# Half products of keys and values moved between the turns of an autocorrelation, and three reorderings, in a two-layer Flamingo block

## The chip, the cores and the metric

The kernel runs on one core of a Trainium2 chip. The metric is the device time of one execution in microseconds (us); the kernel before takes 3443.58 us, the median of three runs (3438.86 to 3445.33).

The engines are named as in the profile: PE is TensorE's matmul, PEld its weight load, DVE is VectorE, ACT is ScalarE, POOL is GpSimd, SP is SyncE. Everything is computed in float32.

## The reference, cut to what matters

The input `x` is 8 batches of 256 rows of 1024, the context `ctx` likewise. Four residual steps follow one another, each on the layer norm of the current `x` and each weighted by the tanh of a gate:

```python
x = x + tanh(g_xattn[0]) * autocorrelation(layernorm(x), ctx, ctx)
x = x + tanh(g_ffn[0])   * lora_ffn(layernorm(x), ...)
x = x + tanh(g_xattn[1]) * attention(layernorm(x), ctx, ctx, mask, wq, wk, wv, wo)
x = x + tanh(g_ffn[1])   * fourier_ffn(layernorm(x), ...)
```

The first is the one that the change is mostly about. For each column it correlates queries and keys over the 256 positions with a Fourier transform, takes the eleven largest lags, weighs them with a softmax, and sums the values shifted by these lags. The second is a dense layer with a low-rank part whose rank is picked for each row by a small gate. The third is attention with 32 query heads on 8 key heads; its keys and values are `ctx @ wk` and `ctx @ wv`, which depend on nothing computed before. The fourth is a dense layer whose weights are folded with a Fourier part.

## The kernel before, in words

The batches are done in two passes of four. In each pass the four steps follow one another on the same eight tiles `xt` of 128 rows, which stay on the chip.

**Products by sevens.** The large matrix products are done by a scheme of seven products in the place of eight (`left_operands` and `right_operands` make sums of quarters; `combine` and `add_product` put the results together). The order of the seven is `SEVEN = (1, 2, 6, 7, 4, 5, 3)`. Products 6, 5, 3 and 7 need sums of weights; in the first pass these are made on the chip (DVE for keys, POOL for values) and stored, and in the later ones they are loaded.

**Keys and values beside the autocorrelation.** `keys_values` computes the keys and values of the third step ahead of time. It is a generator: each of its steps is one half product, eight PE instructions of 128x256. A block of 512 rows has four units (two of keys, two of values) of 14 half products, and a pass has two blocks: 112 half products. In the first pass `fold_last_layer`, which folds the weights of the fourth step, comes behind them with 17 further steps. `autocorrelation` takes steps from this stock with `fill(n)`; what is left when it ends is run without anything beside it. PE has work to do in a fill whatever the autocorrelation waits for. The sums of a product's halves for a key end in a rotary embedding (`rope`, three DVE operations and one on POOL).

**Turns.** The autocorrelation runs over eight half batches (a batch, and 512 of its 1024 columns), one in each call of `turn`, and a ninth call finishes the last. A turn holds two things that belong to different half batches. For its own half batch it does the discrete Fourier transforms of keys and queries (`dft`, L412), their products (`products`, DVE L428 to L431 and POOL L432 to L436, which gives `re` and `im`), the correlation back (`correlation`, L561 and L562, in two parts of two column groups each), and the lags and weights of each of four column groups (`lags`), which end in a tile `both` (POOL L552 and L553). For the half batch before, it transposes `both` (L515), transforms it, multiplies it with the transforms of the values, and goes back to positions: this is `back(l)`, whose two calls each do two matmuls of `inv2` (L531) on the tiles `er`, `ei`, `odr` and `odi`, and add the result to two tiles of `x` (DVE L371). In the order that the products leave POOL these four are `er`, `ei`, `odr`, `odi` (the page names the first two `re` and `im`).

**Order.** Each engine goes through its instructions in the order in which the built program has them. That order follows the source, but a scheduler of the framework moves instructions of one engine past others where it expects a wait, so a step that the source has later isn't always later on its engine. DMAs are nearly all issued from SP's queue[...]. PSUM has two buffers for the products of keys and values, four for `dft`, one for correlations, one for `po` and `pt`.

**Names of the steps.** Ahead of the first turn a pass does `late()`, which loads tiles 2 to 7 of `x` (six DMAs of 512 KB); `normalize(0, 1)`, the statistics of batch 0; and `sums`, which makes the normalized columns and the sums and differences that the transforms start from. After the first turn come the statistics of the other batches, `normalize(1, BP)`.

**The gate of the second step.** `lora_ffn` takes two tiles of rows at a time. `prepare` normalizes and transposes a tile, multiplies it by the low-rank matrix and the gate (`pa`, L623), and masks the result (`xa`, DVE L630 to L642); `turned` transposes `xa` on PE (`px`, L647) and copies it to `xaT`; `left` makes the sums of the tile pair; `project` is the seven products (L670) of the pair before.

Of the kernel before, what the change touches and what calls it, by code (L numbers as in the profile page):

```python
# [11 lines left out]
F32 = mybir.dt.float32  # L12
# [3 lines left out]
ALU = mybir.AluOpType  # L16
# [3 lines left out]
P = 128  # L20
# [9 lines left out]
R0 = 64  # L30
# [9 lines left out]
KH = KC // 2  # L40
# [6 lines left out]
def flamingo_kernel(ctx: ExitStack, tc: tile.TileContext, a: dict, out: bass.AP):  # L47
    nc = tc.nc
# [21 lines left out]
    tg_x, ntg_x = ([t[:, i, 0:1] for i in range(2)] for t in (tg, ntg))  # L70
# [37 lines left out]
    def big_tile(group, shape, name):  # L108
        return big.tile([P, *shape], F32, tag=group, name=name)
# [93 lines left out]
    def left_operands(eng, q, s1, s2, s4):  # L203


        eng.tensor_add(s1, q[1][0], q[1][1])
        eng.tensor_sub(q[1][0], q[0][0], q[1][0])
        eng.tensor_sub(s2, s1, q[0][0])
        eng.tensor_sub(s4, q[0][1], s2)
        return {1: q[0][0], 2: q[0][1], 3: s4, 4: q[1][1], 5: s1, 6: s2, 7: q[1][0]}  # L210
# [158 lines left out]
    def residual(xs, ps, g):  # L369

        nc.vector.scalar_tensor_tensor(xs, ps, g, xs, ALU.mult, ALU.add)  # L371
# [12 lines left out]
    def autocorrelation(p, xt, pools, beside, late):  # L384
        c1, w1, w2, ps_dft, ps_cor, ps_out = pools

        def fill(n):
            for _ in range(n):
                next(beside, None)
# [83 lines left out]
        def turn(this, before, coming):  # L473


            after = None
            if this:
                b, cols, end, qe, qo, ke, ko = this
                if coming:
                    coming = loads(coming)  # L480
                kr_ps, ki_ps = dft((KCE, ke)), dft((KSE, ko), (NYQ, ke))


                kr, ki, kn = sb("kr"), sb("ki"), sb("kn")
                nc.scalar.copy(kr, kr_ps)
                nc.scalar.copy(kn, kr_ps)
                nc.scalar.activation(ki, ki_ps, AF.Copy, scale=pair)
                nc.scalar.copy(kn[0:1, :], ki_ps[0:1, :])
                re, im = sb("re"), sb("im")
                products(spectrum((CE, SE), (qe, qo)), kr, ki, kn, re, im, False)  # L490
                fill(2)

            if this:
                vr_ps, vi_ps = dft((KCO, ko)), dft((KSO, ke))
                vr, vi = sb("vr"), sb("vi")
                nc.scalar.copy(vr, vr_ps)
                nc.scalar.copy(vi, vi_ps)

                nc.vector.scalar_tensor_tensor(
                    kr[0:1, :], end[0:1, :], 2.0 * S, kr[0:1, :], ALU.mult, ALU.add  # L500
                )
                if coming:
                    after = sums(*coming)
                fill(2)
            last = not this
            if before:
                if last:
                    fill(3)
                b_cols, b_tiles, (bkr, bki, bkn, bvr, bvi, both) = before

                wt = []
                for t in range(2):
                    pt = ps_out.tile([P, HALF], F32, tag="out", name="pt")
                    for c in range(4):
                        nc.tensor.transpose(pt[:, c * P : (c + 1) * P], both[:, t, c, :], ident)  # L515
                    wt.append(one(f"wt{t}"))
                    nc.scalar.copy(wt[t], pt)
                    fill(2 if last else 1)
                er, ei = sb("re"), sb("im")
                products(spectrum((CE, SE), wt), bkr, bki, bkn, er, ei, True)  # L520
                fill(2 if last else 1)
                odr, odi = one("odr"), one("odi")
                products(spectrum((CO, SO), wt[::-1]), bvr, bvi, bvr, odr, odi, True)
                fill(3 if last else 1)

            def back(l):

                if before:
                    po = ps_out.tile([P, HALF], F32, tag="out", name="po")
                    for i, (k, sp) in enumerate(((0, er), (3, odi)) if l == 0 else ((1, ei), (2, odr))):  # L530
                        nc.tensor.matmul(po, inv2[:, k, :], sp, start=(i == 0), stop=(i == 1))  # L531
                    residual(b_tiles[0][:, b_cols], po, tg_x[0])
                    residual(b_tiles[1][:, b_cols], po, ntg_x[0] if l else tg_x[0])
                    fill(1)

            if last:
                back(0)
                back(1)
                return None, None
            w = big_tile("xn", [4, S], "w")  # L540
            cor = correlation(re, im, 0)
            fill(1)
            back(0)
            cor += correlation(re, im, 2)
            for c in range(2):
                lags(w[:, c, :], cor[c])
            fill(1)
            back(1)
            for c in range(2, 4):
                lags(w[:, c, :], cor[c])  # L550
            both = big_tile("xn", [2, 4, P], "both")
            nc.gpsimd.tensor_add(both[:, 0], w[:, :, 0:P], w[:, :, P:S])  # L552
            nc.gpsimd.tensor_sub(both[:, 1], w[:, :, 0:P], w[:, :, P:S])  # L553
            return after, (cols, xt[b * 2 : b * 2 + 2], (kr, ki, kn, vr, vi, both))
# [12 lines left out]
        def lags(w, cor):  # L567


            top = w2.tile([P, 16], F32, tag="top", name="top", bufs=4)  # L570
            left = w2.tile([P, S], F32, tag="left", name="left", bufs=1)
            took = w2.tile([P, S], F32, tag="took", name="took", bufs=1)
            nc.vector.max(top[:, 0:8], cor)
            neg = w2.tile([P, 1], F32, tag="neg", name="neg", bufs=4)
            nc.vector.tensor_scalar(neg, top[:, 0:1], -1.0, None, ALU.mult)
            ex = w2.tile([P, S], F32, tag="ex", name="ex")
            nc.scalar.activation(ex, cor, AF.Exp, bias=neg)
            nc.vector.match_replace(left, top[:, 0:8], cor, NEG)
            nc.vector.max(top[:, 8:16], left)
            nc.vector.memset(top[:, 11:16], NEG)  # L580
            nc.vector.match_replace(took, top[:, 8:16], left, NEG)
            tot = w2.tile([P, 1], F32, tag="tot", name="tot", bufs=4)
            nc.vector.scalar_tensor_tensor(
                w, took, NEG, ex, ALU.is_equal, ALU.mult, accum_out=tot
            )
            nc.vector.reciprocal(tot, tot)
            nc.scalar.activation(w, w, AF.Copy, scale=tot)

        order = [(b, h) for b in range(BP) for h in range(2)]
        first = loads(order[0])  # L590
        inv = c1.tile([P, 2, S], F32, name="inv")
        nc.sync.dma_start(inv, a["dft_inv"])
        inv2 = c1.tile([P, 4, P], F32, name="inv2")
        nc.sync.dma_start(inv2, a["lag_inv"])
        late()
        fill(6 if p == 0 else 4)
        normalize(0, 1)
        this, before = sums(*first), None
        fill(7 if p == 0 else 3)
        for i in range(len(order)):  # L600
            this, before = turn(this, before, order[i + 1] if i + 1 < len(order) else None)
            if i == 0:
# [4 lines left out]
    def lora_ffn(xt, w0, make_w0, ag, bl, beside):  # L607

        with (
# [32 lines left out]
                    nc.vector.tensor_scalar(xa[:, r], pa[:, r], past[:, i : i + 1], None, ALU.mult)  # L642
                return xnT, xa

            def turned(xnT, xa):
                px = ps_s.tile([R0 + 1, P], F32, tag="s", name="px")
                nc.tensor.transpose(px, xa, ident)  # L647
                xaT = w2.tile([R0 + 1, P], F32, tag="xaT", name="xaT", bufs=4)
                nc.scalar.copy(xaT, px)
                return xnT, xaT  # L650

            def left(m, first, second):
                q = [[s[0][:, k * KH : (k + 1) * KH, :] for k in range(2)] for s in (first, second)]
                s = [w2.tile([P, KH, P], F32, tag=f"s{i}", name=f"s{i}") for i in (1, 2, 4)]
                ops = left_operands(nc.gpsimd if m else nc.vector, q, *s)
                neg = w2.tile([R0 + 1, P], F32, tag="neg", name="neg")
                nc.vector.tensor_scalar(neg, second[1], -1.0, None, ALU.mult)
                return ops, first[1], second[1], neg

            def project(m, ops, up, low, neg):  # L660
                x = [
# [26 lines left out]
            pending = None  # L688
            for m in range(TT // 2):
                norm = norm_stats(xt[m * 2 : m * 2 + 2])  # L690
                got = [prepare(m * 2 + i, norm) for i in range(2)]
                steps = project(*pending) if pending else iter(())
                for _ in range(2):
                    next(steps, None)
                got = left(m, *(turned(*x) for x in got))
                if pending is None and make_w0:
                    w0.update(make_w0())
                for _ in steps:
                    pass
                pending = (m, *got)  # L700
            beside(w2, ps_t, "t")
            for _ in project(*pending):
                pass
# [444 lines left out]
    for p in range(NPASS):  # L1148
        ga, gb = ("a", "b") if p % 2 == 0 else ("b", "a")
        xt = [xpool.tile([P, D], F32, tag="x", name="x") for t in range(TT)]  # L1150
        with (
# [22 lines left out]
            steps = beside()  # L1174
# [178 lines left out]
```

## Time and profile before

| | before |
|---|---|
| median of three runs | 3443.58 us |
| the profiled execution | 3440.27 us |
| its span in the profile | 3438.5 us |
| mean granted clock of TensorE | 0.984 |
| PE busy | 3335.6 us (97%) |
| DVE, POOL, ACT busy | 2227.5, 1413.8, 860.5 us |
| autocorrelation of the first pass, first transform to last `po` | 36.95 to 396.5 us |
| of the second pass | 1771.37 to 2112.6 us |

A line of the list of waits has the engine and line that waited, what ended the wait, the sum in us, how often, and the longest. A line of the timeline has its start, its duration (of all its instructions together), the engine, line and operation, the tiles and how many; in brackets stands the idle time before it and what ended that. A line of the table of stretches has, for each engine, the busy time and the number of instructions, then the clock granted to TensorE (1.00 is full), the share of DMA and GB/s.

### The profile page before, as it was taken

The page shows a single profiled execution, that of the slowest core. Times are in us where ns is not written, and L with a number is a line of the kernel's source. Part 1 is how long each engine was busy: PE and PEld are TensorE (multiplying, and loading weights), DVE is VectorE, ACT ScalarE, POOL GpSimd, SP SyncE. Part 2 cuts the span into 40 slices and gives each one's busy share as a digit, 9 for nine tenths or more (in the row PEclk, how much of TensorE's full clock was granted, in tenths as well). Part 3 has the DMA queues.
Part 4 walks back from the last instruction along what each step waited for, and adds up shares of the span by engine and source line. Part 5 has one row for each costly group of instructions (what it writes and reads, how often), then busy time and mean ns, then how long its engine had stood idle before and what let it go on. Part 6 is the DMA issues. An engine that isn't in the chain of part 4 may idle for free. (4 is left out here: it accounts for less than half of the span.)

```text
span 3438.5 us, 36954 instructions
## 1 busy us (share of the span) xinstructions
PE 3335.6 (97%) x12784; PEld 2287.7 (67%) x12784; DVE 2227.5 (65%) x4181; ACT 860.5 (25%) x2061; POOL 1413.8 (41%) x1259
## 2 busy tenths in 40 slices
PE   7899989999999999999999999999999999999998
PEld 6576545877766776776466666477777776776754
DVE  7677555877777666666557675456666666666562
ACT  2232101222222322223123321122222322222220
POOL 3665222343443344344546542323443344344443
PEclk9899889999999999999999999999999999999999
DMA  7343533333333333343153334053333333333411
GB/s 266 117 141 108 189 144 128 127 137 135 135 135 125 121 117 124 119 160 112 62 193 116 135 114 148 0 178 114 119 123 116 117 119 123 120 117 126 156 38 49
DMA packets 161864, 431.72 MB, mean 126 GB/s; under 512 B 21476, under 2 KB 56292, under 8 KB 161678
## 3 DMA queue, kind: packets, MB, share of 16 engines
q1 hardware_dynamic: 160526, 425.17, 36.7%
q0 software_dynamic: 1152, 4.19, 0.3%
q8 instruction: 102, 1.67, 0.2%
q14 instruction: 84, 0.69, 0.1%
HBM read 350.66 MB, written 78.64 MB: 125 GB/s over the span
## 5 line engine op out<-in xcount | busy, mean ns | idle before, releaser
L715 POOL TENSOR_TENSOR qT<-rope,rope 128x512 f32<-128x512 f32 x128 | 170.1, 1329 | 864.9 <-DVE rope L714 864.9
L950 PE MATMUL po<-wo,oT 128*128 128x512 f32 x960 | 432.1, 593 | 0.0
L921 PE MATMUL ps_q<-xn,wq 128*128 128x256 f32 x1920 | 428.9, 379 | 0.0
L371 DVE SCALAR_TENSOR_TENSOR x<-po,tg,x 128x512 f32<-128x512 f32 x376 | 268.8, 745 | 227.1 <-PE po L950 70.6
L921 PEld LDWEIGHTS ps_q<-xn,wq 128*128 128x128 f32 x1920 | 365.0, 190 | 50.3 <-PE po L679 0.5
L983 ACT ACTIVATE s<-s,nmx 128x256 f32<-128x256 f32 x512 | 255.9, 500 | 275.1 <-DVE nmx L980 274.6
L978 DVE COPY_PREDICATED s<-keep,ps_s 128x512 f32<-128x512 uint8 x256 | 186.1, 730 | 182.4 <-PE ps_s L969 178.9
L950 PEld LDWEIGHTS po<-wo,oT 128*128 128x128 f32 x960 | 177.5, 190 | 175.5 <-issue 170.4
L950 PE MATMUL po<-wo,oS 128*128 128x512 f32 x640 | 287.7, 593 | 0.3 <-DVE x L371 0.3
L921 PE MATMUL ps_q<-xn_t,wq 128*128 128x256 f32 x1280 | 285.6, 379 | 0.0
L1010 ACT COPY wT<-pt 128x512 f32<-128x512 f32 x256 | 138.0, 590 | 516.3 <-PE pt L1004 516.3
L921 PEld LDWEIGHTS ps_q<-xn_t,wq 128*128 128x128 f32 x1280 | 243.3, 190 | 33.0
L1015 PE MATMUL av<-wT,v 128*128 128x256 f32 x1024 | 247.7, 385 | 2.9 <-ACT wT L1010 2.9
L969 PE MATMUL ps_s<-kT,qT 128*128 128x256 f32 x1024 | 248.1, 379 | 0.0
L1015 PEld LDWEIGHTS av<-wT,v 128*128 128x128 f32 x1024 | 192.4, 191 | 78.0 <-issue 43.9
L992 DVE TENSOR_SCALAR s<-s,tot 128x256 f32<-128x256 f32 x512 | 219.6, 469 | 7.7
L977 POOL MEMSET s<- 128x512 f32 x256 | 129.9, 527 | 223.0 <-PE pt L1004 221.3
L950 PEld LDWEIGHTS po<-wo,oS 128*128 128x128 f32 x640 | 119.0, 190 | 136.6 <-issue 128.9
L969 PEld LDWEIGHTS ps_s<-kT,qT 128*128 128x128 f32 x1024 | 192.0, 190 | 25.4 <-DVE x L371 0.5
L258 POOL TENSOR_TENSOR x<-x,part 128x512 f32<-128x512 f32 x80 | 114.8, 1435 | 196.4 <-ACT part L257 196.4
L980 DVE TENSOR_REDUCE nmx<-s 128x2 f32<-128x512 f32 x256 | 175.0, 685 | 8.3
L263 POOL TENSOR_TENSOR x<-x,part 128x512 f32<-128x512 f32 x80 | 102.9, 1287 | 166.9 <-DVE part L371 143.7
(259 smaller groups left out, 5643.1 us busy)
## 6 DMA issues: line engine op xcount, KB each, us to landing
wq<-in_wq_dram SPq DMA_DIRECT2D x104, 512.0 KB, 3.3
wo<-in_wo_dram SPq DMA_DIRECT2D x104, 512.0 KB, 3.4
wq<-wq_d SPq DMA_DIRECT2D x96, 512.0 KB, 3.2
wo<-wo_d SPq DMA_DIRECT2D x96, 512.0 KB, 3.2
w<-w_d SPq DMA_DIRECT2D x36, 512.0 KB, 4.5
wk<-in_wk_dram SPq DMA_DIRECT2D x26, 512.0 KB, 5.4
wv<-in_wv_dram SPq DMA_DIRECT2D x26, 512.0 KB, 4.1
wk<-wk_d SPq DMA_DIRECT2D x24, 512.0 KB, 3.8
```

The lines of the kernel that those rows point to most:

```text
L371: nc.vector.scalar_tensor_tensor(xs, ps, g, xs, ALU.mult, ALU.add)
L715: nc.gpsimd.tensor_add(dst, t0, t1)
L921: nc.tensor.matmul(ps[:, l, :], wops[r][:, l, c, :], xo[r][:, c, :], start=(c == 0), stop=(c == KH - 1),)
L950: nc.tensor.matmul(po, ops[r][:, h, t * P : (t + 1) * P], wops[r][:, h, :], start=(h == 0), stop=(h == 1),)
L969: nc.tensor.matmul(ps[:, t, :], qT[i, n][:, l, t * P : (t + 1) * P], kT[:, n * S : (n + 1) * S], start=True, stop=True,)
L977: nc.gpsimd.memset(s, MASKED)
L978: nc.vector.copy_predicated(s, keep[b], ps)
L980: nc.vector.tensor_reduce(nmx, s, AX.X, ALU.max, negate=True)
L983: nc.scalar.activation(s[:, t, :], s[:, t, :], AF.Exp, bias=nmx[:, t : t + 1], accum_out=tot[:, t : t + 1],)
L992: nc.vector.tensor_scalar(s[:, t, :], s[:, t, :], tot[:, t : t + 1], None, ALU.mult)
L1010: nc.scalar.copy(wT[i], pt)
L1015: nc.tensor.matmul(av[:, i, :], kv[step][1][:, n * 2 + c, :], wT[i][:, c, :], start=(c == 0), stop=(c == 1),)
```

## The change

It has five parts.

1. *Stock.* Ahead of the first turn `fill(12)` and `fill(9)` take 21 steps in both passes, where it was 6 and 7 in the first pass and 4 and 3 in the second; one step is taken before that in either. In a turn with a half batch before it, two fills of 2 become fills of 1. In the first turn, the second of these becomes 6.
2. *`late()`* comes after the first fill, not ahead of it.
3. *Order of `back`.* Both calls now come after both parts of the correlation.
4. *Order of its parts.* `back(0)` takes `ei` and `odr`, `back(1)` takes `er` and `odi`.
5. *Gates.* In `lora_ffn`, the sums of `left` come first; `turned` and the negative `neg` come after three further steps of `project`.

```diff
@@ turn
-                fill(2)
+                fill(1 if before else 2)
...
-                fill(2)
+                fill(1 if before else 6)
...
             def back(l):
                 if before:
                     po = ps_out.tile([P, HALF], F32, tag="out", name="po")
-                    for i, (k, sp) in enumerate(((0, er), (3, odi)) if l == 0 else ((1, ei), (2, odr))):
+                    for i, (k, sp) in enumerate(((0, er), (3, odi)) if l else ((1, ei), (2, odr))):
                         nc.tensor.matmul(po, inv2[:, k, :], sp, start=(i == 0), stop=(i == 1))
                     residual(b_tiles[0][:, b_cols], po, tg_x[0])
-                    residual(b_tiles[1][:, b_cols], po, ntg_x[0] if l else tg_x[0])
+                    residual(b_tiles[1][:, b_cols], po, tg_x[0] if l else ntg_x[0])
                     fill(1)
...
             cor = correlation(re, im, 0)
             fill(1)
-            back(0)
             cor += correlation(re, im, 2)
             for c in range(2):
                 lags(w[:, c, :], cor[c])
             fill(1)
-            back(1)
+            back(0)
             for c in range(2, 4):
                 lags(w[:, c, :], cor[c])
+            back(1)
@@ autocorrelation
+        fill(12)
         late()
-        fill(6 if p == 0 else 4)
         normalize(0, 1)
         this, before = sums(*first), None
-        fill(7 if p == 0 else 3)
+        fill(9)
@@ lora_ffn
                 for _ in range(2):
                     next(steps, None)
-                got = left(m, *(turned(*x) for x in got))
+                ops = left(m, *(x[0] for x in got))
                 if pending is None and make_w0:
                     w0.update(make_w0())
+                for _ in range(3):
+                    next(steps, None)
+                up, low = (turned(x[1]) for x in got)
+                neg = w2.tile([R0 + 1, P], F32, tag="neg", name="neg")
+                nc.vector.tensor_scalar(neg, low, -1.0, None, ALU.mult)
                 for _ in steps:
                     pass
-                pending = (m, *got)
+                pending = m, ops, up, low, neg
```

`left` and `turned` no longer pass the transposed gate along; `left` returns only the operands of the seven products.

More of the change, by code (lines that the diff above doesn't have):

```diff
@@ L643, in prepare, with turned @@
                 return xnT, xa
-            def turned(xnT, xa):
+            def turned(xa):
                 px = ps_s.tile([R0 + 1, P], F32, tag="s", name="px")
@@ L649, in turned @@
                 nc.scalar.copy(xaT, px)
-                return xnT, xaT
+                return xaT
             def left(m, first, second):
-                q = [[s[0][:, k * KH : (k + 1) * KH, :] for k in range(2)] for s in (first, second)]
+                q = [[s[:, k * KH : (k + 1) * KH, :] for k in range(2)] for s in (first, second)]
                 s = [w2.tile([P, KH, P], F32, tag=f"s{i}", name=f"s{i}") for i in (1, 2, 4)]
[L655 to L658, printed above, removed]
+                return left_operands(nc.gpsimd if m else nc.vector, q, *s)
             def project(m, ops, up, low, neg):
```

## The prediction

> **What bounds the kernel now.** I read the page first, for the engine that is always busy:
>
> ```profile
> PE 3335.6 (97%) x12784; PEld 2287.7 (67%) x12784; DVE 2227.5 (65%) x4181; ACT 860.5 (25%) x2061; POOL 1413.8 (41%) x1259
> PEclk9899889999999999999999999999999999999999
> ```
>
> PE is the bound; its instructions don't change in number. What can be won is its idle time, 3438.5 - 3335.6 = 103 us, and what it loses where the clock is below full, which is in the first sixth above all. So the list of PE's waits came next:
>
> ```profile
> PE po L531 <- POOL odi L434: 18.1, 8, 5.4
> PE po L531 <- POOL re L432: 11.7, 4, 9.2
> PE px L647 <- DVE xa L642: 10.4, 6, 1.7
> ...
> PE ps_cor L561 <- POOL re L432: 5.7, 1, 5.7
> ...
> PE ps_cor L562 <- POOL im L436: 2.9, 1, 2.9
> ```
>
> The edits aim at four of these rows, 38.4 us, and in name at the third. The timeline of PE shows the largest:
>
> ```profile
> 48.81 1.22 PE L561 MATMUL ps_cor<-inv,re 128*128 128x256 f32 x2 [5.68 <-POOL re L432]
> 52.92 1.22 PE L562 MATMUL ps_cor<-inv,im 128*128 128x256 f32 x2 [2.89 <-POOL im L436]
> ...
> 105.91 2.08 PE L531 MATMUL po<-re,inv 128*128 128x512 f32 x2 [9.24 <-POOL re L432]
> 113.37 2.08 PE L531 MATMUL po<-odi,inv 128*128 128x512 f32 x2 [5.39 <-POOL odi L434]
> ```
>
> The first turn has no fill between its transforms and its correlation. In the second, `back(0)` comes too soon. POOL's timeline says why its tiles are late:
>
> ```profile
> 96.20 2.49 POOL L158 TENSOR_TENSOR wv_s<-wv_s,wv 128x512 f32<-128x512 f32 x2
> 98.64 1.27 POOL L238 TENSOR_TENSOR u<-u,m 128x512 f32<-128x512 f32 x1
> 99.86 1.27 POOL L240 TENSOR_TENSOR c<-w,m 128x512 f32<-128x512 f32 x1
> ...
> 108.25 3.39 POOL L158 TENSOR_TENSOR wv_s<-wv,wv_s 128x512 f32<-128x512 f32 x2
> 111.61 1.71 POOL L434 TENSOR_TENSOR odi<-ma,mb 128x512 f32<-128x512 f32 x1
> ```
>
> Sums of value weights stand ahead of `c`; a rope on DVE waits for `c` (12.10 us at 101.16), and `er`'s products stand behind that rope. Last, two later turns, as stretches:
>
> ```profile
> 205.86:243.79 37.93, 37.93 (x152) 27.77 (x151) 28.11 (x71) 11.31 (x21) 20.40 (x16) 1.00 0.39 129
> 243.79:286.88 43.09, 40.15 (x152) 28.77 (x151) 36.35 (x87) 14.88 (x26) 23.26 (x17) 0.96 0.35 110
> ```
>
> A turn without waits takes 37.93 us, all PE. The second has DVE busy for 36.35.
>
> [...] the clock is 0.50 from 50 to 55 and from 100 to 115 us, and the same matmuls take 1.22 us there and 0.59 later. [...] the rope's 64x512 part takes 0.69 us alone and 1.66 beside POOL.
>
> **The change part by part.** A half product is 1.73 us of PE (eight instructions; sixteen take 3.45 from start to start). Nothing is added or removed: it is a matter of what covers what. All sums are against the profiled execution, 3440.27 us, which lies 3.31 below the median.
>
> *Stock and first turn, first pass.* Ahead of the first transform PE now has 22 half products for 14, and 8 in the first turn ahead of its correlation for none: 13.8 us, where 5.68 + 2.89 was waited. Gone are 8.6 us, 0.55 at 29.94 us, and the half clock behind: 32 matmuls took 9.10 for 7.07 us, and two correlation pairs 1.22 for 0.59, so 3.3. Sum 12.4. New: the second unit of keys starts at 36.95, right behind the first. Its third product needs sums that DVE makes from loaded weights. SP issues those loads ahead of the six of `x` now (they were behind them, at 33.3 to 39.5 us). On DVE I count from the row for `c` (ready near 38): two ropes of 2.1, an evacuation of 0.7, five half sums of 0.64, so about 46, and PE asks at 43.9. That is 2 us of wait; where the loads land as slowly as before (9.3 us) or the sums take the 1.7 us each that they took beside POOL at 52.89, 8. I take 4. Next, the product after the first correlation waits for a PSUM buffer, whose evacuation on DVE stands behind `ke`, and that on POOL behind three weight sums: 13 operations of POOL of 1.27 from 60 us on end near 76, PE asks at 74.4; 1.6. Net 12.4 - 5.6 = 6.8.
>
> *The loads of `x`.* Six of 512 KB are issued at about 42 us, after the store of the third key, and land by about 52 (they took 8.6). On DVE their statistics stand ahead of evacuations, whose products PE asks for at 57 and later. I cost this at nothing; the new half products cover it. Without that cover each us of lateness is one of PE.
>
> *Second turn.* Gone are 9.24 + 5.39 and the half clock behind (two `po` pairs 2.08 for 1.02, one half product 3.62 for 1.89, 0.4 after): 18.8. In the changed order no rope stands between `er`'s products on DVE, and the value sums of this unit are done a turn earlier. They now stand ahead of the first `both`: 18 operations of POOL after `re`, 23 us, so it starts near 90, and PE asks at 90.5; I charge 0.3. Net 18.5.
>
> *`back` later, odd part first, all turns.* Between the second spectrum and the first `po` PE had two half products and one correlation (5.2 us); now two and two (6.9), and the first part no longer needs the last tile. `odi` gets a half product and a `po` more: 10.3 us in all, where its longest wait outside the second turn was 2.6 behind 5.2 + 0.9. First pass: 2.09 + 0.39 + 2.56, and 3.6 of half clock. Second: 1.40 + 1.58 + 0.70 + 1.67 + 1.36 + 2.58 + 0.85 = 10.1, and two stretches of half clock (1942 to 1952, 1993 to 1997), 5.4. Sum 24.1.
>
> The lags of the first two column groups start 3.4 us closer to the second part, but from that part to the transpose of `both` PE has 18.0 us in both orders, and `both` was there 2.6 to 7.7 us early in the clean turns. I charge this with the next.
>
> *Shorter turns.* Twelve half products become ten: 37.93 - 3.45 = 34.48 us of PE. A turn of values needs DVE for 23.6 to 25.8 us: hidden. A turn of keys needs 28.1 to 36.4, less about 1.7 for two half products (five evacuations and four ropes, 11.9 us in 14): up to 34.7 against 34.48. It just fits[...]. I charge 2 us in each of the four turns full of keys, 8.
>
> *End.* The second pass runs out of stock (116 wanted, 112 there), so its last four fills are empty: `back` then waits for POOL by about 1 us, less than its shortest cover. In the first pass two more steps of the fold run after the last `po`; before, PE ran at half clock from 410 to 447 us in this narrow work (40 rows)[...]. I charge 3 together.
>
> *Gates.* Nothing. In the changed program's order `px` stands on PE between the same matmuls as before, and so do `xa`'s operations on DVE around it; the scheduler had moved it there already. The six waits of 1.7 are the second DVE row of `xa`[...] and stay.
>
> Sum: 6.8 + 18.5 + 24.1 - 8 - 3 = 38.4. The profiled execution would take 3402, the median 3405 us.
>
> **Rivals.**
> *All of it and more (about 3380).* The key turns fit, and other waits of the stretch (3.02 on `c`, 1.83 on `both`, 1.52, 1.88) go too: 38.4 + 8 + 8 + 5.6 + 3 = 63. For it: value turns have room. Against: it needs every new cover to hold.
> *Half of it (about 3424).* The first unit's new waits reach 8 us [...], and the transpose of `both` waits in most turns: 38 less 4, 3 and 14 turns of 0.9. For it: `both` had only 2.6 us to spare at 254. Against: the 18.0 us are unchanged.
> *The gates do what they say (about 3394).* The six waits go, 10.4 more. Against: the order.
> *Slower: DVE becomes the bound of the turns.* If DVE and POOL set a turn's length, the 28 half products taken out of 14 turns are 48 us that leave idle gaps there. The gain without the charge for turns, 46 us, is spent when a mean turn is 3.3 us longer than its 34.48, 37.8. At 38.5 the time is 3443.6 + 10 = 3453. Against: the clean value turns would need 40% more DVE time.
>
> **Chances.** Forecast 0.52, all and more 0.20, half 0.17, gates 0.03, slower 0.04, and 0.04 for no change within 0.2% (7 us), which is about what a measurement of this kernel can tell. Faster by over 0.2%: 0.52 + 0.20 + 0.17 + 0.03 = 0.92. The range holds the forecast, the gates, most of half and of all and more: 3378 to 3428.
>
> **What would show it.** The rows `po <- odi` and `po <- re` under 4 us together, no wait at the two `ps_cor` rows, `px <- xa` still 10.4; a clean turn of 34.5 us; the first transform near 53 to 57 us and behind a wait on `wk_s`; full clock from 60 to 400 us. I am wrong if waits of `ps_k` or `ps_v` on DVE, or of `pt` on `both`, grow past 20 us, or if the statistics of `x` hold up DVE in the first turn.

## The result and the profile after

The changed kernel takes 3455.26 us, the median of seven runs (3449.29 to 3456.58); the kernel before took 3440.8 us beside it (seven runs, 3436.0 to 3445.33). The ratio is 1.0037, 95% interval 1.0026 to 1.0049: slower by 0.4%. The forecast was 3405 us, with 0.92 on faster. The profiled execution took 3455.26 us, with a span of 3453.5 us, 15.0 us longer than the span before.

The engines' totals and the clock, from the page of the changed kernel:

```profile
PE 3346.2 (97%) x12784; PEld 2289.6 (66%) x12784; DVE 2230.5 (65%) x4181; ACT 861.1 (25%) x2061; POOL 1412.7 (41%) x1259
PEclk9999889999999999999999999999999999999999
```

PE is idle for 107.3 us (102.9 before) and busy for 10.6 us more with the same instructions. The clock accounts for the second: laid over PE's timeline, the record of the clock has PE busy at half clock for 105.1 us, for 85.2 before; by estimate, half of the difference, 10.0 us, is what the halved clock costs (the pairs of correlation matmuls in the kernel before took 1.22 us at half clock and 0.59 at full). The list of waits says where the idle time went:

```profile
PE po L532 <- DVE x L371: 17.8, 11, 5.3
PE px L648 <- DVE xa L643: 10.4, 6, 1.7
PE po L532 <- DVE top L581: 10.3, 4, 4.3
PE ps_v L797 <- DVE c L244: 10.0, 4, 3.6
...
PE ps_v L797 <- DVE u L231: 7.8, 2, 4.0
...
PE ps_k L797 <- DVE wk_s L158: 3.3, 1, 3.3
...
PE ps_k L797 <- DVE v L244: 1.5, 1, 1.5
...
PE ps_k L797 <- DVE c L244: 1.0, 1, 1.0
...
PE ps_k L797 <- DVE w L234: 0.5, 1, 0.5
```

The four rows that the edits aimed at are gone: no `po` waits for POOL, no `ps_cor` waits at all. In their place stand 28.1 us of `po` waiting for DVE, in 15 places. The waits of `ps_k` and `ps_v` on DVE's evacuations (the rows on `c`, `u`, `v` and `w`) have grown from 7.0 to 20.8 us. In the kernel before they were:

```profile
PE ps_v L794 <- DVE c L244: 3.0, 1, 3.0
...
PE ps_k L794 <- DVE v L244: 1.9, 1, 1.9
...
PE ps_k L794 <- DVE c L228: 1.5, 1, 1.5
...
PE ps_k L794 <- DVE w L234: 0.6, 1, 0.6
```

The timeline of PE shows two of this second kind:

```profile
81.15 3.59 PE L797 MATMUL ps_v<-wv,cx 128*128 128x256 f32 x8 [3.61 <-DVE c L244]
...
109.20 3.78 PE L797 MATMUL ps_v<-wv,cx_t 128*128 128x256 f32 x8 [3.89 <-DVE u L231]
```

By stage, from the starts of matmuls in the two timelines (the fold's second half begins with the first matmul of L320, the gated step with the first `pa`, the attention with the first `ps_q`):

| | before, us | after, us | change |
|---|---|---|---|
| to the second half of the fold | 403.5 | 402.3 | -1.2 |
| from there to the attention | 184.2 | 189.8 | +5.6 |
| attention and fourth step, first pass | 1169.8 | 1171.4 | +1.6 |
| second pass, to its first `pa` | 363.8 | 370.8 | +7.0 |
| the rest | 1317.2 | 1319.2 | +2.0 |

So the first pass gave back nearly all that it won. The second pass, for which the forecast had 15.5 us from the order of `back` alone (10.1 of waits and 5.4 of half clock), lost 7.0.

**The second part's output buffer.** The longest wait of the first kind in the first pass is one of 5.11 us. This is its place, in the timeline of all engines but PE's weight loads:

```profile
235.26 1.02 PE L532 MATMUL po<-im,inv 128*128 128x512 f32 x2
...
236.12 1.02 PE L532 MATMUL po<-odr,inv 128*128 128x512 f32 x2
...
236.97 3.62 PE L797 MATMUL ps_k<-cx,wk 128*128 128x256 f32 x16
...
243.46 0.69 DVE L717 TENSOR_TENSOR rope<-c,tab 64x512 f32<-64x512 f32 x1
...
244.26 0.73 DVE L371 SCALAR_TENSOR_TENSOR x<-po,tg,x 128x512 f32<-128x512 f32 x1
...
244.91 0.74 DVE L371 SCALAR_TENSOR_TENSOR x<-po,ntg,x 128x512 f32<-128x512 f32 x1
...
245.70 2.07 PE L532 MATMUL po<-re,inv 128*128 128x512 f32 x2 [5.11 <-DVE x L371]
```

`re` and `odi` have been ready since 233. What the second part lacks is its PSUM buffer: `po` has one, and the first part's result is still in it. That result is complete at 237.14. DVE then still has the lags of two column groups, an evacuation and a rope ahead of the two residuals, which end at 245.65. PE asked at 240.59. The same place in the kernel before:

```profile
235.78 1.39 DVE L371 SCALAR_TENSOR_TENSOR x<-po,tg,x 128x512 f32<-128x512 f32 x2
...
240.34 1.02 PE L531 MATMUL po<-im,inv 128*128 128x512 f32 x2
```

There the residuals ended at 237.17, ahead of a part of the second column group's lags and of the evacuation and rope. PE asked only at 240.34, with a correlation and two half products between the parts. The four waits put down to `top` are the same wait: at 203.72 the matmul starts as the residual ends (202.93 + 0.74), and the name is that of an instruction which follows it on DVE.

**The correction of `ke`.** The other kind, POOL, DVE and PE together around 109 us:

```profile
104.30 1.26 POOL L436 TENSOR_TENSOR im<-mb,ma 128x512 f32<-128x512 f32 x1
105.52 1.26 POOL L461 TENSOR_TENSOR ke<-cn 128x512 f32<-128x512 f32 x1
...
106.81 1.73 DVE L467 SCALAR_TENSOR_TENSOR ke<-end,ke 128x512 f32<-128x512 f32 x1 [6.05 <-POOL ke L461]
...
108.47 0.68 DVE L231 TENSOR_TENSOR u<-ps_v,u 128x512 f32<-128x512 f32 x1
109.20 3.35 PE L797 MATMUL ps_v<-wv,cx_t 128*128 128x256 f32 x7 [3.89 <-DVE u L231]
```

DVE stands idle for 6.05 us in front of `ke`'s correction, which waits for a sum that POOL makes as its seventh in a row. Behind it on DVE is the evacuation `u`, which has had its data for long, and PE waits for the buffer that `u` empties. DVE isn't short of time: in the turn that has the wait of 5.11 us it is busy for 29.5 of 41.6 us, the last line of these:

```profile
133.77:168.91 35.14, 34.74 (x136) 24.64 (x135) 24.33 (x68) 10.98 (x20) 17.59 (x14) 1.00 0.49 172
168.91:207.67 38.76, 36.43 (x135) 25.23 (x134) 25.95 (x71) 14.66 (x25) 29.29 (x23) 0.96 0.36 116
207.67:249.28 41.61, 36.50 (x136) 25.27 (x134) 29.47 (x73) 11.96 (x22) 21.66 (x17) 0.95 0.36 114
```

These are three turns in the table of stretches (of the engines' columns the third is DVE's); without waits each would take 34.5 us.

### The profile page after: what moved, and what is told of

The parts are those of the page before. It is cut to its first block, busy times and chain, and to the rows that moved or that the text cites. A ratio compares the mean times of both kernels' runs of the same rounds, so it can differ in the third digit from the quotient of the medians.

```text
span 3453.5 us, 36964 instructions
## 1 busy us (share of the span) xinstructions
PE 3346.2 (97%) x12784; PEld 2289.6 (66%) x12784; DVE 2230.5 (65%) x4181; ACT 861.1 (25%) x2061; POOL 1412.7 (41%) x1259
## 5 line engine op out<-in xcount | busy, mean ns | idle before, releaser
L972 PEld LDWEIGHTS ps_s<-kT,qT 128*128 128x128 f32 x1024 | 191.6, 190 | 25.3 <-DVE x L371 0.5
L263 POOL TENSOR_TENSOR x<-x,part 128x512 f32<-128x512 f32 x80 | 102.9, 1288 | 168.3 <-DVE part L371 144.1
```

The source lines that it names most:

```text
L972: nc.tensor.matmul(ps[:, t, :], qT[i, n][:, l, t * P : (t + 1) * P], kT[:, n * S : (n + 1) * S], start=True, stop=True,)
```

## The experiments

Three theories. *Theory 1*: the single output buffer of `po` makes the second part wait for the first part's residuals. *Theory 2*: ten half products a turn are too few for DVE's amount of work. *Theory 3*, formed after the first four runs: the order on DVE, namely `ke`'s correction, holds up evacuations. Each row has the median and the ratio to the kernel before on the same chip. The kernels ran on several chips, on which the kernel before took 3440.8 to 3443.0 us, so 2 us between two rows say nothing:

| kernel | us | ratio (95%) |
|---|---|---|
| changed | 3455.3 | 1.0037 (1.0026 to 1.0049) |
| gates undone | 3455.4 | 1.0033 (1.0023 to 1.0043) |
| stock alone | 3447.9 | 1.0018 (1.0011 to 1.0024) |
| order alone | 3447.8 | 1.0011 (1.0002 to 1.0019) |
| changed, parts swapped in place | 3442.0 | 0.9996 (0.9987 to 1.0005) |
| changed + own buffer | 3440.2 | 0.9990 (0.9983 to 0.9997) |
| the same, second pass with the stock of before | 3429.6 | 0.9964 (0.9950 to 0.9978) |
| order + own buffer, old stock | 3422.5 | 0.9945 (0.9928 to 0.9961) |
| changed + `ke` off DVE | 3430.4 | 0.9967 (0.9953 to 0.9981) |
| changed + own buffer + `ke` off DVE (ACT) | 3412.6 | 0.9917 (0.9901 to 0.9934) |
| the same, scaling on DVE | 3420.4 | 0.9933 (0.9917 to 0.9950) |
| the same with ACT, fold ahead | 3412.0 | 0.9912 (0.9895 to 0.9928) |
| the same with ACT, old stock | 3432.4 | 0.9970 (0.9959 to 0.9982) |
| changed + own buffer + `ke` all on POOL | 3414.8 | 0.9922 (0.9902 to 0.9942) |
| the same, old stock | 3426.5 | 0.9956 (0.9940 to 0.9971) |
| the same, old stock in the second pass only | 3420.5 | 0.9938 (0.9918 to 0.9958) |

### The first part gets its own buffer

```diff
@@ back, on the changed kernel
-                    po = ps_out.tile([P, HALF], F32, tag="out", name="po")
+                    po = (ps_out if l else ps_dft).tile([P, HALF], F32, tag="out" if l else "dft", name="po")
```

> The changed kernel, but the tile po of the first part comes from the pool of the spectra (four PSUM buffers) where the second part keeps the only output buffer; the same instructions otherwise. Theory 1 (one output buffer: the second part's first matmul waits for the residual of the first part, which DVE takes late): the rows po waiting for DVE x or DVE top, 28.1 us in the changed kernel, fall below 5 us and take some 5 to 10 us of half clock with them, so 3415 to 3425 us, faster than both kernels. Theory 2 (ten half products a turn are too few to cover DVE, whichever buffer is waited for): these rows turn into waits of ps_k, ps_v, pt or dft on DVE of about the same sum, and the time stays at 3445 to 3455 us.

Measured: 3440.2 us, 15 us less than the changed kernel, and all 28.1 us of `po` on DVE are gone. The timeline of the same place:

```profile
233.44 1.02 PE L532 MATMUL po<-im,inv 128*128 128x512 f32 x2
...
236.89 1.02 PE L532 MATMUL po<-re,inv 128*128 128x512 f32 x2
...
241.24 0.73 DVE L371 SCALAR_TENSOR_TENSOR x<-po,tg,x 128x512 f32<-128x512 f32 x1
```

The second part no longer waits for the residual of the first, which comes 4 us after it. But half or more of what theory 1 promised is missing, and theory 2's sign is there too; in the list of waits:

```profile
PE ps_v L797 <- DVE c L244: 11.8, 4, 4.0
...
PE ps_v L797 <- DVE u L231: 7.9, 2, 4.0
PE ps_k L797 <- DVE w L234: 7.7, 3, 4.2
```

With smaller rows the waits on DVE's evacuations are now 33.5 us (20.8 in the changed kernel). At the largest of them:

```profile
1952.73 0.69 DVE L467 SCALAR_TENSOR_TENSOR ke<-end,ke 128x512 f32<-128x512 f32 x1 [7.39 <-POOL ke L461]
...
1953.34 0.68 DVE L234 TENSOR_TENSOR w<-ps_k,u 128x512 f32<-128x512 f32 x1
...
1954.08 3.02 PE L797 MATMUL ps_k<-cx_t,wk 128*128 128x256 f32 x8 [4.19 <-DVE w L234]
```

DVE was idle for 7.39 us before it, 86.4 us in all sixteen such places. That speaks for its order, not its amount: theory 3.

### Stock alone, order alone, gates undone

Stock alone is the changed kernel with `back` as before (so it has the new place of `late()` and the gates' edit too); order alone is the kernel before with the changed `back`:

```diff
@@ order alone, turn, on the kernel before
-            back(0)
             cor += correlation(re, im, 2)
...
             fill(1)
-            back(1)
+            back(0)
             for c in range(2, 4):
                 lags(w[:, c, :], cor[c])
+            back(1)
```

(with the parts and signs of the changed kernel). In the kernel with the gates undone the last hunk of the diff, `lora_ffn`, is taken back.

> The changed kernel with the two parts put back: places, order and signs as in the kernel before, so only the stock of half products (and the gates) is changed. Theory 1: no wait of po on DVE above 2 us in all; the rows po on POOL odi and re come back in the later turns with some 10 to 20 us; 3425 to 3440 us. Theory 2 (turns too short for DVE): 3450 to 3460 us, with waits of ps_k and ps_v on DVE above 25 us.

> The kernel before with the two parts' places, order and signs of the changed one; twelve half products a turn and the gates as before. Theory 1: the waits of po on POOL (29.8 us) go but waits of po on DVE of 20 to 30 us take their place, 3435 to 3450 us. Theory 2 (the order is good and only the short turns cost): waits of po below 8 us in all, about 3415 us.

> The changed kernel with the gates' edit undone. If that edit does nothing, as forecast: within 4 us of the changed kernel, and px waiting for DVE xa 10.4 us as in both kernels. If it costs something: 5 us or more below the changed kernel.

Each half of the change is slower by itself. With the stock alone `po` waits on POOL for 10.4 us, as theory 1 has it, but the evacuations make PE wait for 29 us, as theory 2 has it, and 3447.9 lies between both. With the order alone theory 1's waits are there in twelve-product turns also:

```profile
PE po L531 <- DVE top L580: 17.4, 5, 6.3
PE po L531 <- DVE x L371: 13.2, 9, 4.2
```

30.6 us, where the kernel before waited for POOL for 29.8: the forecast gain of the order was spent on the buffer. The gates' edit is worth nothing, as forecast: 3455.4 for 3455.3, and the six waits of `px` are 10.4 us in both.

### The parts swapped, but left at their places

```diff
@@ turn, on the changed kernel
             cor = correlation(re, im, 0)
             fill(1)
+            back(0)
             cor += correlation(re, im, 2)
...
             fill(1)
-            back(0)
+            back(1)
             for c in range(2, 4):
                 lags(w[:, c, :], cor[c])
-            back(1)
```

> The changed kernel with the two parts at the places of the kernel before (the first between the two correlations), but in the changed order, odd part first; one output buffer. Theory 1 (one output buffer): with a correlation and a half product between the parts the waits of po on DVE fall from 28 us to below 4 us; theory 1 adds that the swap spares odi's lateness, so po waits for POOL below 5 us (10.4 us with the stock alone): 3438 to 3443 us. If the swap does nothing: po on POOL 10 us, and 3448 us as with the stock alone.

3442.0 us: with a correlation between the parts one buffer is enough (`po` on DVE 3.8 us, on POOL 4.2). The swap by itself is worth 6 us against the stock alone, and the move costs 13 us.

### The order with its own buffer

The kernel before with both diffs, that of the order and that of the buffer.

> The kernel before with the changed places and order of the two parts, and the first part's own PSUM buffer; the stock and the gates as before. It measures the gain that the forecast gave to the new order, 24 us, where the output buffer is not in its way. Theory 1: the 30.6 us of waits of po on DVE that the order alone had are gone, the one of 7 us on im stays; 3415 to 3425 us. If another wait takes their place: 3435 to 3445 us.

3422.5 us, 20 us less than before, where the forecast had given this term 24.1. The order does what it is meant to once the buffer is out of its way.

### The second pass with the stock of before

```diff
@@ turn and autocorrelation, on the changed kernel with its own buffer
-                fill(1 if before else 2)
+                fill(2 if p else 1 if before else 2)
...
-                fill(1 if before else 6)
+                fill(2 if p else 1 if before else 6)
...
-        fill(12)
+        fill(4 if p else 12)
         late()
...
-        fill(9)
+        fill(3 if p else 9)
```

> The kernel with the first part's own buffer; in the second pass, whose first turn had no wait before, the stock is as in the kernel before (8 half products ahead of the first transform, 12 a turn). If the shorter turns are what costs in the second pass: its stretch from the start of the pass to the first pa falls from 364 to about 348 us, 3420 to 3427 us in all. If they cost nothing: 364 us again and 3440 us.

3429.6 us; the second pass to its first `pa` takes 355.0 us for 364.0. So the changed stock costs 9 us in the second pass as long as DVE's order is as it was, a little over half of the 16 that I expected. DVE is idle at `ke`'s correction for as long in this pass with either stock (46.9 and 46.1 us), but the waits on its evacuations are 8.0 us for 15.6: twelve half products hide what ten don't.

### `ke`'s correction off DVE

```diff
@@ sums and turn, on the changed kernel with its own buffer
-            nc.vector.scalar_tensor_tensor(ke, end, -2.0, ke, ALU.mult, ALU.add)
+            nc.scalar.activation(end, end, AF.Copy, scale=-2.0)
+            nc.gpsimd.tensor_add(ke, ke, end)
...
-                    kr[0:1, :], end[0:1, :], 2.0 * S, kr[0:1, :], ALU.mult, ALU.add
+                    kr[0:1, :], end[0:1, :], -1.0 * S, kr[0:1, :], ALU.mult, ALU.add
```

> The kernel with the first part's own buffer, and the correction of ke taken from DVE: ACT scales the row end by -2 in place, POOL adds it (and kr takes end times -S for 2S). Theory 3 (DVE stands in order behind the correction of ke, which waits for POOL, and the evacuation behind it holds a PSUM buffer that PE waits for): the waits of ps_k and ps_v on DVE w, u and c at the places of 3 to 4.2 us, 26.6 us in all in the kernel with its own buffer, fall below 8 us, and some half clock goes with them: 3405 to 3418 us. Rival (DVE's sum of work is what is too long for ten half products): the same waits come back at other evacuations, and 3435 to 3442 us.

3412.6 us, 0.9917 of the kernel before: with the variant that moves the fold (3412.0, below) the fastest here. The waits on evacuations fall from 33.5 to 3.9 us; a wait on ACT now leads the list:

```profile
PE pt L516 <- ACT wt L518: 10.7, 4, 3.7
...
PE ps_v L798 <- DVE c L244: 2.2, 2, 1.3
...
PE ps_k L798 <- DVE c L244: 1.2, 1, 1.2
...
PE ps_k L798 <- DVE w L234: 0.5, 1, 0.5
```

With the changed kernel's one buffer:

> The changed kernel with its one output buffer, and only the correction of ke taken from DVE. If the two causes add: the waits of po on DVE stay at 20 to 30 us and those of ps_k and ps_v at the correction (17 us here) go, 3430 to 3438 us. If the correction was also what made the residuals late: po's waits fall below 10 us too, and 3412 to 3420 us.

3430.4 us, and its waits for the output buffer stay at 25.6 us:

```profile
PE po L533 <- DVE x L371: 18.0, 11, 4.3
...
PE po L533 <- DVE top L582: 7.6, 4, 3.3
```

So the two causes add up, nearly: alone they are worth 15 and 25 us, together 43 (3455.3 to 3412.6). To tell the wait from the work, the scaling was put on DVE, with the form of instruction that had been taken away:

```diff
@@ sums, on the kernel with both repairs
-            nc.scalar.activation(end, end, AF.Copy, scale=-2.0)
+            nc.vector.scalar_tensor_tensor(end, end, -1.0, end, ALU.mult, ALU.subtract)
```

> As the kernel with its own buffer and the correction off DVE, but the scaling of the row end by -2 is done by DVE and not ACT, with the same form of instruction (128x512, one scalar, two tensors) that the correction had: DVE has as much work as in the changed kernel and only waits no more for POOL there. Theory 3 (the wait in order is what costs): 3408 to 3418 us, as without it. Rival (it was DVE's amount of work, 16 instructions of 0.7 to 1.7 us): 3425 to 3440 us.

3420.4 us, between the two forecasts and nearer to theory 3's. DVE now does all its former work again (2227.7 us busy, 2226.1 in the kernel with its own buffer) and 20 of the 28 us stay won: it was mostly the waiting. Even here DVE waits at that line, for the load of `end`, 41.6 us in all where it was 86.4 for POOL. Whether the other 8 us are this wait or DVE's work isn't shown. Theory 2 falls as the main cause.

### What the stock is worth without the obstacles

The old stock with both repairs is the kernel before with the order, the own buffer and `ke`'s correction changed. With ACT it went the other way than expected:

> The kernel with the order changed and the first part's own buffer, the stock as before, and the correction of ke taken from DVE (ACT scales, POOL adds). With the stock of before that correction should cost less, since twelve half products a turn cover it: its waits there were some 10 us (5.9, 2.5, 1.9 and 0.9), so 3408 to 3416 us. The kernel with the changed stock and the same two repairs took 3412.6 us: if the stock is worth anything once the repairs are made (forecast 17 us for the first two turns), this one is 5 us or more above it; if it is within 4 us, the stock is worth nothing.

3432.4 us, 10 us slower than without the repair of `ke`. This is ACT and PE in its second pass:

```profile
1814.48 0.63 ACT L467 ACTIVATE end<-end 128x512 f32<-128x512 f32 x1 [9.26 <-DMA end<-in_ctx_dram]
...
1815.01 0.57 ACT L518 COPY wt<-pt 128x512 f32<-128x512 f32 x1
1815.63 2.07 PE L412 MATMUL dft<-wt,mats 128*128 128x512 f32 x2 [6.28 <-ACT wt L518]
```

The waiting instruction had been moved to ACT, and now stood ahead of a copy that PE needs. The kernel with the changed stock has this wait too: it is the row of 10.7 us above. So the correction was put on POOL as a whole, where its input comes from, by two subtractions of `end`:

```diff
@@ sums, on the kernels with their own buffer
-            nc.vector.scalar_tensor_tensor(ke, end, -2.0, ke, ALU.mult, ALU.add)
+            nc.gpsimd.tensor_sub(ke, ke, end)
+            nc.gpsimd.tensor_sub(ke, ke, end)
```

> The kernel with the first part's own buffer; ke's correction is two subtractions of the row end on POOL, so neither DVE nor ACT has an instruction that waits for POOL or for the load of end (POOL has 16 operations more than in the repair with ACT's scaling: 32 for the 16 taken from DVE). Theory 3, extended (whatever engine takes the waiting instruction, what stands behind it is late): the 11.5 us of waits of PE for ACT wt that the repair with ACT had go, the DVE waits stay away: 3396 to 3408 us. Rival (POOL becomes the one that is late): waits on POOL both, re or im of 10 us and more, 3412 to 3425 us.

> The same two repairs with the stock of the kernel before. What the stock is worth without the two obstacles is this time less that of the run with the changed stock. Forecast of the prediction's own terms: first and second turn 25.3 us for the stock, 8 against it, 17 us in all: 3413 to 3425 us here. If the stock is worth nothing once DVE is free: within 4 us of the other.

> The same two repairs, changed stock in the first pass and the stock of before in the second. If ten half products a turn are enough once DVE is free, the second pass gains or loses nothing by it (its stretch 349 us in the repair with ACT): within 4 us of the run with the changed stock in both. If the short turns still cost: 5 to 15 us faster than it.

Changed stock 3414.8 us, old stock 3426.5, changed in the first pass only 3420.5. The waits on ACT's `wt` went, as expected, but the time didn't fall; it lies where the rival had it, though by other waits than its own. PE now waits 8.9 us for a buffer of the spectra, in which the first part's `po` lies (at 240.85 for the residual that ends at 240.79), and 4.1 us for `both`:

```profile
PE dft L412 <- DVE x L371: 8.9, 2, 4.6
...
PE pt L516 <- POOL both L554: 4.1, 4, 1.5
```

The stock is worth 12 us, where its own terms in the forecast came to 17. Ten half products a turn are then no worse than twelve. Of the ten full turns after the second turns, six take 34.5 to 35.6 us, two 36.2, and only the two with the wait for `po`'s buffer 42; and the old stock in the second pass isn't faster (355.7 us to its first `pa`, for 351.0). With the old stock, moving the correction to POOL gains nothing: 3426.5 us, where the order and the own buffer alone gave 3422.5. So with twelve half products a turn neither form of this repair is worth anything.

### The fold

```diff
@@ turn, on the kernel with its own buffer and the repair with ACT
-                fill(3 if last else 1)
+                fill(5 if last else 1)
```

> The kernel with both repairs (own buffer, ke off DVE), and in the last turn two more steps of the fold ahead of the two parts, as in the kernel before, so that eight of the narrow matmuls (40 columns) run ahead of the po matmuls and not behind. If their place is why PE stays at half clock longer: the half clock from the end of the fold on falls from 44 to about 37 us, and the time by 2 to 4 us, to 3408.5 to 3410.5 us. If not: 3412 us.

3412.0 us for 3412.6: no effect, and the half clock from the fold to the attention was 44.4 us in both. How far this stage scatters is shown by two kernels whose first passes are the same, instruction for instruction: those with the correction on POOL and the changed stock in both passes, or in the first only. The stretch from the second half of the fold to the attention, in this order:

```profile
385.70:571.10 185.40, 175.10 (x522) 87.41 (x522) 106.05 (x200) 19.13 (x39) 40.37 (x32) 0.88 0.34 124
```

```profile
383.50:573.90 190.40, 177.95 (x521) 88.35 (x521) 106.15 (x200) 19.13 (x39) 40.38 (x32) 0.87 0.33 121
```

The same program took 5.0 us more in the second, with 51.2 for 44.4 us at half clock: PE was busy for 2.9 us more and idle for 2.2 more. So two single profiles can't tell whether the change lengthens this stage by 5.6 us. All the profiles together make some 3 us likely: the stretch takes 184.2 to 186.1 us in the five kernels with the old stock in the first pass (mean 185.4), and 185.4 to 190.9 in the twelve with the changed one (mean 188.6). No run isolates the reason.

## Why the prediction was wrong

- **`back` later, 24.1 us: the step that failed first.** I asked when `re` and `odi` are ready and how much PE has ahead of them, and there I was right: no `po` waits for POOL any more. I didn't ask what else `po` needs. One PSUM buffer serves both parts; I had it in the description of the kernel and not in the sum. The parts came closer (at the place shown, 6.9 us from the start of the first to the asking of the second became 5.3), and the residuals that empty the buffer were put behind lags. The term had to be +24.1 less 28.1 of new waits and the half clock behind them (0.50 from 244.84 to 251.67 us, behind the wait of 5.11); with the buffer free, the order gave 20. In the run in which the first part has a buffer of its own, the 28.1 us of waits are gone.
- **Shorter turns, -8 us: mis-sized, with the wrong reason.** I compared DVE's busy time (34.7) with PE's (34.48) and took 2 us for each of four turns full of keys. Busy time wasn't the measure. The trace of before has DVE idle at `ke`'s correction for 74.2 us in all; with twelve half products that cost PE little. With own buffer and ten, the four turns full of keys took 5.0, 3.8, 6.9 and 4.0 us over 34.47, 20 us and not 8. Three turns that are only in part of keys, for which I charged nothing, took 7.2, 1.9 and 8.6 more. With the correction off DVE (ACT's scaling) these seven lose 17 us in place of 37, hardly any of it to evacuations, and one other turn loses 4.8 us, most of it to ACT's `wt`. The sign that I had named for this, waits of `ps_k` or `ps_v` on DVE above 20 us, came: 20.8. The prediction had DVE stand for 12.10 us at a rope with `er`'s products behind it, and used that order for one wait only.
- **First and second turn, 25.3 us: little over a third of it came.** The third turn starts at 133.77 after ten half products more than before (17.25 us), so 9.4 us were won. The 8.6, the 9.24 and the 5.39 us are gone as forecast, and the wait on `wk_s` is 3.3 where I took 4. New waits were 15.4 us and not 5.9: besides that one 3.6 on `c` at 81 us, 3.9 on `u` at 109, 2.3 on the buffer, 1.2 on `kn` and 1.0 on `c`, the two largest behind `ke`'s correction. And the clock, which I had full from 60 us on, was halved for 10.2 us after that in these two turns. With both repairs (the kernel with ACT's scaling) the third turn starts at 126.69; less the 17.25 that is 109.4 for 125.96: 16.5 us won.
- **End, -3 us,** of which two, for the fold, rested on no trace. Measured -5.6 in one pair of profiles and some -3 over all of them, in a stage that scatters by 5. **Gates, 0, and the loads of `x`, 0:** right for the gates by a run of their own; for the second nothing in the waits speaks against it, but no run moves `late()` alone.
- **The chances.** The rival "DVE becomes the bound of the turns" had 0.04, and its time, 3453 us, was nearly met, as was its mean turn: 38.5 us, where twelve turns of ten half products in the changed kernel took 39.8. That is luck, as its reason was wrong: DVE was busy for only 29.5 of 41.6 us in the turn with the wait of 5.11 us. I had rejected the rival since DVE would need 40% more time; it needed only a different order.

With both repairs the changed kernel is 29 us faster than the kernel before, where I had forecast 38: most of what the prediction counted was there to be won, behind two waits that it did not count.

That the twelve half products a turn had covered the wait at `ke` is shown by the runs (in the second pass 8.0 us of waits on evacuations with twelve, 15.6 with ten). The scheduler places half products a little differently in each kernel; this is part of what each repair measures, and wasn't separated.

## What to carry to other kernels

When work is moved closer together, list all that an instruction needs, its output buffer as well as its operands, and when the buffer's last reader runs on its own engine (here PE asked at 240.59 us and the residual ended at 245.65). Before taking cover away, look for where an engine stands idle ahead of an instruction that waits for another engine, with work behind it that has its data (here DVE, 6.05 us ahead of `ke`'s correction with `u` behind it): its idle time there is what the cover may be hiding, and the busy share of that engine doesn't show it (DVE's was 65% before and after). When such an instruction is moved to another engine, it can take its wait along (10.7 us of PE behind ACT's `wt`), so look at what stands behind it there; here ACT and POOL, where its input is made, came out within 2 us of each other.

## What was not expected of the hardware

Two identical first passes differed by 5.0 us in the fold and the gated step, with 44.4 and 51.2 us at half clock. What makes the difference is not shown. In this stage of the changed kernel the half clock came with PE busy, for 43.3 of 44.4 us (37.1 of 37.5 in the kernel before), mostly in matmuls with 40 rows (L320, 26.5 us) or 68 columns (L624, 8.0 us) and in transposes (L366, 6.4 us).
